# Gated convolution layers: six of eight output blocks by seven half-depth products, and a next layer that begins with two of four chunks

## The chip, the cores and the metric

The kernel runs on one core of a Trainium2 chip. The metric is the device time in microseconds (us) from start to end of one execution; the time given is the median of three runs. Everything is computed in float32.

The engines are called as in the profile: PE multiplies matrices, PEld loads its weights, DVE is the vector engine, ACT the scalar engine, POOL the GpSimd engine, SP an engine that only issues transfers. A name with q (SPq, ACTq) is the engine's queue. Each engine executes its own instructions in the order in which the compiled program has them.

## The reference

The input x is an image of 512 channels and 64 by 64 pixels. Four layers are added to it one after the other, each on the group-normalized image (32 groups of 16 channels, `_gn`):

```
x = x + attention(gn(x))              # layer 0
x = x + gated_convs(gn(x), L1 weights)
x = x + gated_convs(gn(x), L2 weights)
x = x + linear_attention(gn(x))       # layer 3
```

The change is in the two gated layers, and in the seams behind them. A gated layer (channels of `pwa`, `dw0`, `dw1`, `dw2`: 128, 128, 256, 512) is

```
fused  = w_in @ x + b_in              # 1024 x 512
pwa, abc = fused[:128], fused[128:]
dw0, dw1, dw2 = depthwise_7x7(abc) + dw_b
h = pwa * dw0
h = (pw0 @ h + pw0_b) * dw1
h = (pw1 @ h + pw1_b) * dw2
out = w_out @ h + b_out               # 512 x 512
```

The last line, `w_out @ h`, is what the change computes in another way. Layer 3 begins with a 1x1 convolution of the normalized image as well (`w_qkv`, 768 x 512).

## The kernel before, in words

The image X stays in SBUF as four chunks of 128 channels by 4096 pixels; 512 pixels are a block, so there are 8 blocks (`NB`) and 4 chunks (`NC`). A product of one chunk and one block is one matmul of 128 by 128 weights and 512 columns. In float32 the profile records each such matmul twice.

The kernel is written in a language whose scheduler orders instructions from their dependencies and from estimates of their durations. An instruction is placed by hand with `tc.keep_in_program_order`, which puts it behind the last instruction that was traced on the same engine before it. All matmuls that go through `pc.matmul` are placed so: PE follows the order in which the program was traced. Tiles come from pools with a number of buffers; a new tile waits until a buffer of its pool comes free, and a pool of the next layer until what lay there before comes free.

**A gated layer** (`_gated_convs`, once for L1, once for L2). The products of `w_in` are done in pairs of two output chunks and two pixel blocks. `_Seven.steps` does such a pair of pairs in seven products of half depth (two matmuls each) in place of eight, with sums of the weights (`sums`) and differences of the pixels (`differences`, L472); the products p1, p5, p2, p7, p6, p3, p4 follow in this order. Two intermediate results are kept in SBUF (`keep`, on ACT) and added to on DVE (L518, L522). `diff` holds the eight differences of a pair of blocks, in one buffer of the pool `ch` (tiles of 128 by 4096, 5 buffers), from which also the gate `G` and the convolved planes `D[0]` to `D[6]` come.

The seven depthwise convolutions (`convolve(0)` to `convolve(6)`) are done on PE from shifted copies of the planes: each of eight parts of a convolution needs a load of taps (`T`, L1181) and of planes (`S`, L1197) issued by SP, and two copies on ACT (L1204). Two loads are issued ahead, four buffers hold them. Between the parts a list of other products is worked off in order, as many as the number of parts allows: for the last two convolutions these are the gates `g[3]` and `g[4]` (L1475) and the parts of the output product for `D[3]` and `D[4]`, one matmul for each of 8 blocks and 4 output chunks (`output`, L1487 and L1491). When the last convolution is done, `g[5]` and `g[6]` follow and the output product for `D[5]` and `D[6]`, two matmuls each, in the order of the output chunks. As each piece of X is complete, DVE takes its statistics (`bn_stats`, L1493).

**The seam between layers.** The mean and the deviation of a chunk are known when its eight blocks are done. `_Norm.params` combines them in three pieces: the aggregation (L95), a first small matmul with `gmask` (L126) and a second (L135), each followed by small instructions on DVE and ACT. After the second, the factor `r` scales the weights. `centered.take` subtracts the mean from the pixels (L400 on ACT, L401 on the others). The next layer begins in `_first_blocks`, with two output chunks and two blocks, so that three of the four chunks (`NC - 1`) go first: 12 matmuls that need nothing of the last chunk. The pieces for the last chunk are put between them after the fourth and the seventh matmul. Then the last chunk's four matmuls follow.

**The opening of layer 3** (`_linear_attention`). POOL sets the planes of the layer to zero (L1121), issues five transfers into tiles `bt` (L1674) and multiplies four of them (L1680); the result is used later, in `added` (L1684). Then come the scaling of `w_qkv` on DVE (L1693) and `_first_blocks`. Planes are stored by transfers that POOL issues (L1150).

Of the kernel before, what the change touches and what calls it, by code (L numbers as in the profile page):

```python
# [10 lines left out]
FP = mybir.dt.float32  # L11
# [426 lines left out]
class _Seven:  # L438
# [42 lines left out]
    def first(self, a, x, ps):  # L481
        self.multiply(ps, a[:, 0:2], [x(c, 0) for c in range(2)], True)

    def steps(self, a, b, s, t, x, bank, keep, put, early=lambda more, last: None, p1_kept=None):

        nc = self.nc
        ps, kept = {}, {}

        def add(j, w, hs, first):

            if first:
                ps[j] = bank(j)
            self.multiply(ps[j], w, hs, first)

        def p1():
            if p1_kept is not None:
# [12 lines left out]
        def p2():  # L511
            if p1_kept is None:
                add(0, a[:, 2:4], [x(2 + c, 0) for c in range(2)], False)
                put(0, 0, ps[0], None)

        def p7():
            add(2, s[2], t[2], True)
            nc.vector.tensor_add(kept[1], kept[1], ps[2])  # L518

        def p6():  # L520
            add(3, s[1], t[1], True)
            nc.vector.tensor_add(kept[0], kept[0], ps[3])  # L522
            early(kept[0], kept[1])

        def p3():
            add(1, s[3], [x(2 + c, 1) for c in range(2)], False)
            put(0, 1, ps[1], kept[0])

        def p4():
            add(2, b[:, 2:4], t[3], False)  # L530
            put(1, 0, ps[2], kept[0])
            put(1, 1, kept[1], kept[0])

        return [p1, p5, p2, p7, p6, p3, p4]


# [736 lines left out]
                yield  # L1273


def _first_blocks(pc, X, ws, bank, put, pieces, scale, meanwhile):
# [24 lines left out]
    for f in meanwhile:  # L1301
        f()
    for i, k, ps in first:
        add(i, k, ps, NC - 1)
        put(i, k, ps, None)


@with_exitstack
def _gated_convs(ctx, tc, a, X, vcol, vall, gmask, small, new_stats, centered, stats, mv, F):
# [18 lines left out]
    for layer in ("L1", "L2"):  # L1328
# [13 lines left out]
        if norm is None:  # L1342

            norm, ready = _Norm(nc, small, gmask, mv), 0
            centered.by(norm)
            root = wp.tile([1, 1], FP, tag="root", name="root")
            tc.keep_in_program_order(nc.scalar.activation(root, gmask[0:1, 0:1], AF.Sqrt))
            _all(
                norm.params(
                    0, NC, None, bank_gn, centered.first(lambda c: pc.pixels(X[:, c, :], 0))  # L1350
                )
            )
            for c in range(NC):
                centered.scaled(w_in[0], norm.r, nc.vector, c, c + 1, True)
            centered.scaled(w_in[1], norm.r, nc.scalar)
        else:
            ready = NC - 1
# [11 lines left out]
        seven = _Seven(tc, pc.matmul)  # L1369

        def taken(k):
            for c in range(ready if k < 2 else 0, NC):
                centered.take(pc.pixels(X[:, c, :], k), c)

        D = {}

# [53 lines left out]
        def group(i, k):  # L1430
# [7 lines left out]
            def step(n):  # L1438
                if n == 0:
                    if i not in wsum:  # L1440
                        summed(i)
                    steps.extend(
                        seven.steps(
                            w_in[i], w_in[i + 1], wsum[i], diff, view(k), bank,
                            lambda j, ps: keep(i, j, ps),
                            lambda m, n, ps, more: put(i + m, 2 * k + n, ps, more),
                        )
                    )
                    for _ in mine:
                        pass  # L1450
# [11 lines left out]
        def gate(i, b):  # L1462
# [11 lines left out]
                bias = vcol(pre + "pw1_b", i - 3)  # L1474
            nc.vector.scalar_tensor_tensor(d, ps, bias, d, ALU.add, ALU.mult)  # L1475

        def output(chunks, b, o):

            if (b, o) == (0, 0):
                for i in chunks:  # L1480
                    w_out.append(weights("w_out", i - 3))
            ps = product(
                lambda c: w_out[chunks[c] - 3][:, o, :], [D[i][:, ts(b, BLK)] for i in chunks]
            )
            xs = X[:, o, ts(b, BLK)]
            if chunks[0] == 3:
                nc.vector.scalar_tensor_tensor(  # L1487
                    xs, ps, vcol(pre + "b_out", o), xs, ALU.add, ALU.add
                )
            else:  # L1490
                nc.vector.tensor_add(xs, xs, ps)  # L1491
            if chunks[-1] == NDW - 1:
                nc.vector.bn_stats(stats[:, o, b, :], xs)  # L1493


        def blocks(f, i):
            n = (0, 1, 1, 2, 2, 2, 2)[i]
# [54 lines left out]
        _first_blocks(  # L1552
            pc, X, w_in, lambda: ps_mm.tile([P, BLK], FP, tag="mm", name="ps"), put,
            norm.params(ready, NC, old_stats, bank_gn, centered_first) if ready else None,
            scale_last, [] if ready else [lambda: taken(1)],
        )
        centered.began()
        for b in (2, 3):
# [26 lines left out]
        for b, f in enumerate(last[(NC - 1) * NB :]):  # L1585
            f()
            if b in (1, 3):
                next(pieces, None)
        for k in range(2 if layer == "L1" else NB):
            for c in range(NC - 1):  # L1590
                centered.take(_pixels(form, X[:, c, :], k), c)
    return stats, norm

# [2 lines left out]
def _linear_attention(ctx, tc, a, X, vcol, vall, ident, gmask, small, centered, stats, norm, F, Z, out):  # L1596
# [46 lines left out]
    with ExitStack() as st:  # L1643
# [73 lines left out]
            return ps  # L1717

        for i, w in enumerate(w_qkv):
            scaled(i, w, 0, NC - 1)  # L1720
# [58 lines left out]
        def group(i, k, also=()):  # L1779
# [3 lines left out]
            def begin():  # L1783
# [2 lines left out]
                        w_qkv[i], w_qkv[i + 1], wsum[i], diff[k][0], view(k), bank,  # L1786
                        lambda j, ps: keep(i, j, ps),
                        lambda m, n, ps, more: put(i + m, 2 * k + n, ps, more),
                    )
                )  # L1790

# [16 lines left out]
        dve, pool = nc.vector, nc.gpsimd  # L1808

        def centered_first():  # L1810
            tc.keep_in_program_order(
                centered.take(pc.pixels(X[:, NC - 1, :], 0), NC - 1, nc.vector)
            )
            centered.take(pc.pixels(X[:, NC - 1, :], 1), NC - 1)

        def scale_last():
            for i, w in enumerate(w_qkv):
                scaled(i, w, NC - 1)

        _first_blocks(  # L1820
            pc, X, w_qkv, lambda: ps_mm.tile([P, BLK], FP, tag="mm", name="ps"), put,
            norm.params(
                NC - 1, NC, stats,
                lambda: ps_vk.tile([P, BLK], FP, tag="vk0", name="gn_ps"), centered_first,
            ),
            scale_last,
            [lambda: taken(2), lambda: taken(3), lambda: summed(0)] + differences(1, dve),
        )
        centered.began()
        made = group(0, 1, centers(2) + differences(2, dve))  # L1830
# [512 lines left out]
```

## Time and profile before

| what | value |
|---|---|
| median of three runs | 3753.89 us (3752.48 to 3755.92) |
| the profiled execution's own time | 3760.95 us |
| its span, from the first to the last instruction | 3758.9 us |
| granted clock of PE | 0.998 |
| PE busy | 3694.5 us, 98% |
| DVE busy | 2722.7 us, 72% |
| ACT busy | 2067.1 us, 55% |
| POOL busy | 190.3 us, 5% |
| L1: convolution 5 begins, 6 begins, output product ends | 2499.3, 2541.9, 2680.1 us |
| L2: convolution 5 begins, 6 begins, output product ends | 2986.7, 3029.2, 3167.4 us |

A row of a timeline gives the start of a run of equal instructions, how long the run lasted from the start of the first to the end of the last, the engine, the line, the operation, the tiles (out<-in) and their number. What stands in brackets is how long the engine was idle before it, and who released it. A matmul's recorded duration reaches into the next one; the time that a matmul costs is read from the starts. A row of a table by stretches gives the stretch, its length, the busy time of PE, PEld, DVE, ACT and POOL with the number of instructions in brackets, the granted clock of PE, the mean busy share of the 16 DMA engines and what they moved in GB/s.

### The profile page before, as it was taken

What the parts mean: (1) busy time and instruction counts of PE and PEld (TensorE: products, weight loads), DVE (VectorE), ACT (ScalarE), POOL (GpSimd) and SP (SyncE); (2) the same over time, 40 slices, a digit from 0 to 9 for tenths busy, and PEclk for the clock granted to TensorE, in tenths of its full rate; (3) what the DMA queues carried; (4) which work ended last, traced back from release to release, by engine and by line L of the source; (5) the groups of instructions that cost most, each with busy time, mean ns of one, the idle gap of its engine ahead of it and who ended that gap; (6) DMA issues with size and microseconds to landing.
All of it is one profiled execution on the core that took longest, in us unless ns stands there. A gap on an engine that the chain in (4) does not pass through costs nothing. (4 is left out here: it accounts for less than half of the span.)

```text
span 3758.9 us, 81698 instructions
## 1 busy us (share of the span) xinstructions
PE 3694.5 (98%) x35112; PEld 1716.1 (46%) x35112; DVE 2722.7 (72%) x3548; ACT 2067.1 (55%) x3002; POOL 190.3 (5%) x170
## 2 busy tenths in 40 slices
PE   7999999999999999999999999999999999999999
PEld 6544444444464444444333344554444544445543
DVE  6677777777766777778778757776777678666538
ACT  3577774777735777747557546662356632355210
POOL 1000000000000000010000000000000002232112
PEclk9999999999999999999999999999999999999999
DMA  2000000000000000000000026762066631564312
GB/s 102 10 7 7 4 7 12 7 4 7 7 4 10 7 7 4 7 12 7 4 4 7 4 76 199 197 185 60 23 182 187 191 89 41 157 180 104 99 56 93
DMA packets 183469, 222.72 MB, mean 59 GB/s; under 512 B 15800, under 2 KB 124600, under 8 KB 182976
## 3 DMA queue, kind: packets, MB, share of 16 engines
q1 hardware_dynamic: 158896, 158.62, 15.7%
q10 hardware_dynamic: 21168, 47.77, 3.5%
q0 software_dynamic: 3040, 11.08, 0.8%
q8 instruction: 277, 4.54, 0.5%
q14 instruction: 88, 0.72, 0.1%
HBM read 157.51 MB, written 59.90 MB: 58 GB/s over the span
## 5 line engine op out<-in xcount | busy, mean ns | idle before, releaser
L844 ACT ACTIVATE pt<-ps_s,A 128x512 f32<-128x512 f32 x2048 | 1286.1, 688 | 447.1 <-PE ps_s L836 436.9
L836 PE MATMUL ps_s<-O,K 64*64 64x512 f32 x8192 | 1419.8, 589 | 0.0
L1017 DVE TENSOR_TENSOR acc<-acc,pt 128x1024 f32<-128x1024 f32 x960 | 1177.5, 1227 | 324.6 <-ACT pt L844 298.7
L856 PE MATMUL av<-pt,O 64*64 64x512 f32 x4096 | 747.0, 589 | 0.0
L856 PE MATMUL av<-pt,V 64*64 64x512 f32 x4096 | 674.3, 589 | 0.0
L836 PEld LDWEIGHTS ps_s<-O,K 64*64 64x64 f32 x8192 | 438.8, 133 | 513.3 <-issue 463.2
L1204 ACT COPY S<-S 32x1295 f32<-32x1295 f32 (+1 forms) x272 | 341.8, 1257 | 228.7 <-DMA S<-F 137.3
L856 PEld LDWEIGHTS av<-pt,O 64*64 64x64 f32 x4096 | 238.0, 133 | 250.5 <-issue 237.7
L856 PEld LDWEIGHTS av<-pt,V 64*64 64x64 f32 x4096 | 210.1, 133 | 266.9 <-issue 252.1
L1127 PEld LDWEIGHTS ps_cv<-S,T 64*32 64x32 f32 x13824 | 194.0, 105 | 115.7 <-issue 72.5
L1127 PE MATMUL ps<-diff,w_sum 128*128 128x512 f32 x516 | 242.0, 601 | 3.5 <-DVE w_sum L459 2.9
L1127 PE MATMUL ps_cv<-S,T 64*32 64x128 f32 x13824 | 234.6, 273 | 9.0 <-issue 4.2
L1127 PE MATMUL ps<-h,w_out_L 128*128 128x512 f32 x512 | 229.6, 600 | 1.6 <-DVE X L1487 1.4
L472 DVE TENSOR_TENSOR diff<-X 128x512 f32<-128x512 f32 x200 | 134.9, 691 | 68.0 <-PE ps L1127 36.1
L400 ACT ACTIVATE X<-X,gn_less 128x512 f32<-128x512 f32 x118 | 75.3, 709 | 153.7 <-DVE gn_less L130 153.0
L1127 PE MATMUL ps<-X,w_in_L 128*128 128x512 f32 x304 | 146.2, 612 | 10.9 <-ACT kept L1409 7.8
L1127 PEld LDWEIGHTS ps<-diff,w_sum 128*128 128x128 f32 x516 | 94.6, 190 | 117.3 <-issue 104.0
L1127 PEld LDWEIGHTS ps<-h,w_out_L 128*128 128x128 f32 x512 | 94.0, 190 | 118.3 <-issue 96.5
L1127 PE MATMUL ps<-h,pw_L 128*128 128x512 f32 x320 | 144.3, 600 | 3.0 <-DVE h L1475 2.8
L1258 DVE STREAM_TRANSPOSE h<-ps_cv 128x512 f32<-128x512 f32 x112 | 109.2, 1048 | 52.3 <-PE ps_cv L1127 52.0
L472 DVE TENSOR_TENSOR diff<-X,diff 128x512 f32<-128x512 f32 x200 | 135.3, 685 | 11.6 <-PE ps L1127 11.5
L1127 PE MATMUL ps<-agg,w_proj 128*128 128x512 f32 x256 | 117.2, 595 | 1.6 <-DVE turned L1258 1.6
(265 smaller groups left out, 3354.2 us busy)
## 6 DMA issues: line engine op xcount, KB each, us to landing
T<-in_L_T_dram SPq DMA_DIRECT2D x112, 384.0 KB, 4.2
F<-plane ACTq DMA_DIRECT2D x112, 324.0 KB, 3.5
S<-F SPq DMA_DIRECT2D x224, 162.0 KB, 4.7
S<-G SPq DMA_DIRECT2D x96, 153.0 KB, 4.5
row<-G SPq DMA_DIRECT2D x48, 272.0 KB, 3.4
T<-in_L_T_dram SPq DMA_DIRECT2D x48, 256.0 KB, 4.2
G<-plane POOLq DMA_DIRECT2D x33, 289.0 KB, 2.7
rd<-R SPq DMA_DIRECT2D x64, 128.0 KB, 2.9
```

The costliest lines, as they stand in the source:

```text
L400: return self.nc.scalar.activation(xs, xs, AF.Identity, bias=less)
L472: yield eng.tensor_tensor(t[j][c], a(c), b(c), ALU.subtract)
L836: nc.tensor.matmul(ps[ts(half, D), ts(h, BLK)], K[rows, t * P + half * D : t * P + (half + 1) * D], QO[pair][rows, cols], start=True, stop ...
L844: exp = nc.scalar.activation(pt[:, ts(h, BLK)], ps[:, ts(h, BLK)], AF.Exp, bias=A[:, t, h : h + 1])
L856: nc.tensor.matmul(av[half][rows, :], v[keys, t * P + h * D : t * P + (h + 1) * D], pt[keys, ts(h, BLK)], start=(t == 0), stop=(t == NT - 1),)
L1017: add = nc.vector.tensor_add(acc, acc if u > 1 else first, pt)
L1127: self.tc.keep_in_program_order(self.nc.tensor.matmul(*args, **kw))
L1204: nc.scalar.copy(second, first)
L1258: nc.vector.transpose(out, src)
```

## The change

In both gated layers the output product is no longer split by the depth of `D`, with one part behind each of the last convolutions, for all blocks. Blocks 0 and 1 are done as before, behind the same convolutions. Blocks 2 to 7 are done after them, as three pairs of blocks with all four of `D[3]` to `D[6]`, by `_Seven.steps` for two output chunks at a time (`outputs_by_seven`). The sums of `w_out` are made on POOL, the differences on DVE, the kept results are copied by ACT. Where a result has a second summand, POOL adds it to X (in the last group of all DVE does), and then DVE takes the statistics. `w_out` is loaded as four tiles by output chunk instead of by depth, before convolution 5. Because `D[3]` to `D[6]` now all live to the end, the pool `ch` has six buffers.

Chunks 2 and 3 of X are now complete only at the end of the last group. So the next layer begins with two chunks (`READY`) instead of three: 8 matmuls, then, in place of the four that are missing, the first products (p1) of the groups that follow (`begin_two` in L2 for two groups, `begin_one` in layer 3 for one), then 8 matmuls of chunks 2 and 3. The centering of the first two chunks is prepared for the blocks 0, 1, 2 and 4 (`FIRST`) in L2. Chunk 2 of the first block is centered on POOL, chunk 3 on DVE; in layer 3 POOL centers chunk 2 of the later blocks too.

```diff
@@ _Seven.steps, p1
-            ps[0] = bank(0)
-            self.first(a, x, ps[0])
+            if given is None:
+                ps[0] = bank(0)
+                self.first(a, x, ps[0])
+            else:
+                ps[0] = given
             kept[0] = keep(0, ps[0])
@@ _first_blocks
-    for n, (i, k, ps, c) in enumerate((*p, c) for p in first for c in range(NC - 1)):
+    for n, (i, k, ps, c) in enumerate((*p, c) for p in first for c in range(READY)):
         add(i, k, ps, c)
         if n in (3, 6):
             next(pieces, None)
+    early()
     scale()
     for f in meanwhile:
         f()
     for i, k, ps in first:
-        add(i, k, ps, NC - 1)
+        for c in range(READY, NC):
+            add(i, k, ps, c)
         put(i, k, ps, None)
+READY = 2
+FIRST = (0, 1, 2, 4)
@@ _gated_convs
-    hp = ctx.enter_context(tc.tile_pool(name="ch", bufs=5))
+    hp = ctx.enter_context(tc.tile_pool(name="ch", bufs=6))
...
+        def begin_two():
+            for k in (1, 2):
+                begun[k] = ps_cv.tile([P, BLK], FP, tag="mm", name="ps7")
+                seven.first(w_in[0], view(k), begun[k])
...
+        def load_out():
+            for o in range(NC):
+                t = w2p.tile([P, NC, P], FP, tag="w", name=f"w_out_{layer}")
+                nc.sync.dma_start(
+                    out=t, in_=a[f"{layer}_w_out"][:, :, o].rearrange("c p m -> p c m")
+                )
+                w_out.append(t)
...
+        def outputs_by_seven(ks):
+            diff = hp.tile([P, N], FP, tag="h", name="diff")
+            diff = [[diff[:, ts(2 * j + c, BLK)] for c in range(2)] for j in range(4)]
+            rest = hp.tile([P, N], FP, tag="h", name="rest")
...
+            for m in range(2):
+                _all(seven.sums(nc.gpsimd, w_out[2 * m], w_out[2 * m + 1], sums[m]))
...
+            for k in ks:
...
+                made = seven.differences(nc.vector, view, diff)
+                for m in range(2):
+                    def add(i, n, first, more):
+                        o, b = 2 * m + i, 2 * k + n
+                        xs = X[:, o, ts(b, BLK)]
+                        nc.vector.scalar_tensor_tensor(
+                            xs, first, vcol(pre + "b_out", o), xs, ALU.add, ALU.add
+                        )
+                        if more is not None:
+                            eng = nc.vector if (k, m) == (ks[-1], 1) else nc.gpsimd
+                            eng.tensor_tensor(xs, xs, more, ALU.add)
+                        nc.vector.bn_stats(stats[:, o, b, :], xs)
...
+                    for n, step in enumerate(steps):
+                        if m == 0:
+                            for _ in range((2, 2, 2, 0, 2, 0, 0)[n]):
+                                next(made)
+                        step()
+                        yield
...
-                (n, lambda b=b, o=o: output(chunks, b, o)) for b in range(NB) for o in range(NC)
+                (n, lambda b=b, o=o: output(chunks, b, o)) for b in range(2) for o in range(NC)
...
         def centered_first():
-            tc.keep_in_program_order(
-                centered.take(pc.pixels(X[:, NC - 1, :], 0), NC - 1, nc.vector)
-            )
-            centered.take(pc.pixels(X[:, NC - 1, :], 1), NC - 1)
+            for c in range(READY, NC):
+                tc.keep_in_program_order(
+                    centered.take(
+                        pc.pixels(X[:, c, :], 0), c, nc.vector if c == NC - 1 else nc.gpsimd
+                    )
+                )
+            for c in range(READY, NC):
+                centered.take(pc.pixels(X[:, c, :], 1), c)
...
         convolve(4, [], b56[16:])
+        load_out()
         convolve(5, g[3], outputs(3))
         convolve(6, [], g[4] + outputs(4))
-        for _, f in g[5] + g[6]:
-            f()
-        last = [lambda b=b, o=o: output((5, 6), b, o) for o in range(NC) for b in range(NB)]
-        for f in last[: (NC - 1) * NB]:
+        for _, f in g[5] + g[6] + outputs(5, 6):
             f()
         norm = _Norm(nc, small, gmask)
         centered.by(norm)
-        pieces = norm.params(0, NC - 1, stats, bank_gn)
-        next(pieces)
+        pieces = norm.params(0, READY, stats, bank_gn)
+        ks = range(1, NB // 2)
+        for n, _ in enumerate(outputs_by_seven(ks)):
+            if n - (14 * len(ks) - 7) in (1, 3, 4):
+                next(pieces, None)
@@ _linear_attention
         def taken(k):
-            centered.take(pc.pixels(X[:, NC - 1, :], k), NC - 1)
+            for c in range(READY, NC):
+                centered.take(pc.pixels(X[:, c, :], k), c, nc.gpsimd if c < NC - 1 else None)
...
+        def begin_one():
+            begun.append(bank(0))
+            seven.first(w_qkv[0], view(1), begun[0])
```

In layer 3 `centered_first` has the same form as in the gated layers, the weights are scaled in two steps of two chunks, and the small matmuls of the normalization take the bank `vk3` instead of `vk0`.

More of the change, by code (lines that the diff above doesn't have):

```diff
@@ L482, in first, with steps @@
         self.multiply(ps, a[:, 0:2], [x(c, 0) for c in range(2)], True)
-    def steps(self, a, b, s, t, x, bank, keep, put, early=lambda more, last: None, p1_kept=None):
+    def steps(self, a, b, s, t, x, bank, keep, put, early=lambda more, last: None, p1_kept=None,
+              given=None):
         nc = self.nc
@@ L1273, in conv, with _first_blocks @@
                 yield
-def _first_blocks(pc, X, ws, bank, put, pieces, scale, meanwhile):
+def _first_blocks(pc, X, ws, bank, put, pieces, scale, meanwhile, early):
     first = [(i, k, bank()) for k in range(2) for i in range(2)]
@@ L1356, in _gated_convs @@
         else:
-            ready = NC - 1
+            ready = READY
             for w in w_in[:2]:
@@ L1371, in taken @@
         def taken(k):
-            for c in range(ready if k < 2 else 0, NC):
+            for c in range(ready if k in FIRST else 0, NC):
                 centered.take(pc.pixels(X[:, c, :], k), c)
+        begun = {}
+        def begin_two():
+            for k in (1, 2):
+                begun[k] = ps_cv.tile([P, BLK], FP, tag="mm", name="ps7")
+                seven.first(w_in[0], view(k), begun[k])
         D = {}
@@ L1446, in step @@
                             lambda m, n, ps, more: put(i + m, 2 * k + n, ps, more),
+                            given=begun.pop(k, None),
                         )
@@ L1475, in gate @@
             nc.vector.scalar_tensor_tensor(d, ps, bias, d, ALU.add, ALU.mult)
+        def load_out():
[5 more added lines that the diff above has]
+                w_out.append(t)
         def output(chunks, b, o):
-            if (b, o) == (0, 0):
-                for i in chunks:
-                    w_out.append(weights("w_out", i - 3))
             ps = product(
-                lambda c: w_out[chunks[c] - 3][:, o, :], [D[i][:, ts(b, BLK)] for i in chunks]
+                lambda c: w_out[o][:, chunks[c] - 3, :], [D[i][:, ts(b, BLK)] for i in chunks]
             )
@@ L1493, in output, with keep, view, put @@
                 nc.vector.bn_stats(stats[:, o, b, :], xs)
+        def outputs_by_seven(ks):
+            diff = hp.tile([P, N], FP, tag="h", name="diff")
+            diff = [[diff[:, ts(2 * j + c, BLK)] for c in range(2)] for j in range(4)]
+            rest = hp.tile([P, N], FP, tag="h", name="rest")
+            sums = rest[:, 0 : N // 2].rearrange("p (m n c k) -> p m n c k", m=2, n=4, c=2)
+            rows = [rest[:, ts(n, BLK)] for n in range(NB // 2, NB)]
+            sums = [[sums[:, m, n] for n in range(4)] for m in range(2)]
+            for m in range(2):
+                _all(seven.sums(nc.gpsimd, w_out[2 * m], w_out[2 * m + 1], sums[m]))
+            def keep(j, ps):
+                t = rows.pop(0)
+                rows.append(t)
+                nc.scalar.copy(t, ps)
+                return t
+            for k in ks:
+                def view(c, n):
+                    return D[3 + c][:, ts(2 * k + n, BLK)]
+                made = seven.differences(nc.vector, view, diff)
[10 more added lines that the diff above has]
+                        nc.vector.bn_stats(stats[:, o, b, :], xs)
+                    def put(i, n, ps, more):
+                        if (i, n) != (1, 1):
+                            add(i, n, ps, more)
+                    steps = seven.steps(
+                        w_out[2 * m], w_out[2 * m + 1], sums[m], diff, view, bank, keep, put,
+                        lambda more, last: add(1, 1, last, more),
+                    )
[5 more added lines that the diff above has]
+                        yield
         def blocks(f, i):
@@ L1542, in centered_first @@
         def centered_first():
-            tc.keep_in_program_order(
-                centered.take(pc.pixels(X[:, NC - 1, :], 0), NC - 1, nc.vector)
-            )
-            centered.take(pc.pixels(X[:, NC - 1, :], 1), NC - 1)
+            for c in range(READY, NC):
[3 more added lines that the diff above has]
+                    )
+                )
+            for c in range(READY, NC):
+                centered.take(pc.pixels(X[:, c, :], 1), c)
         def scale_last():
@@ L1554, in _gated_convs @@
             norm.params(ready, NC, old_stats, bank_gn, centered_first) if ready else None,
-            scale_last, [] if ready else [lambda: taken(1)],
+            scale_last, [] if ready else [lambda: taken(1)], begin_two,
         )
@@ L1581, in _gated_convs @@
         centered.by(norm)
-        pieces = norm.params(0, NC - 1, stats, bank_gn)
-        next(pieces)
-        form = FORM if layer == "L1" else FORM3
[L1585 to L1590, printed above, removed]
+        pieces = norm.params(0, READY, stats, bank_gn)
[3 more added lines that the diff above has]
+                next(pieces, None)
+        form = FORM if layer == "L1" else FORM3
+        for k in FIRST if layer == "L1" else range(NB):
+            for c in range(READY):
                 centered.take(_pixels(form, X[:, c, :], k), c)
@@ L1719, in _linear_attention @@
         for i, w in enumerate(w_qkv):
-            scaled(i, w, 0, NC - 1)
+            scaled(i, w, 0, READY)
         def taken(k):
-            centered.take(pc.pixels(X[:, NC - 1, :], k), NC - 1)
+            for c in range(READY, NC):
+                centered.take(pc.pixels(X[:, c, :], k), c, nc.gpsimd if c < NC - 1 else None)
         def put(i, k, ps, more=None):
@@ L1788, in begin @@
                         lambda m, n, ps, more: put(i + m, 2 * k + n, ps, more),
+                        given=begun.pop() if begun else None,
                     )
@@ L1810, in centered_first @@
         def centered_first():
[L1811 to L1814, printed above, removed]
+            for c in range(READY, NC):
+                tc.keep_in_program_order(
+                    centered.take(
+                        pc.pixels(X[:, c, :], 0), c, nc.vector if c == NC - 1 else nc.gpsimd
+                    )
+                )
+            for c in range(READY, NC):
+                centered.take(pc.pixels(X[:, c, :], 1), c)
         def scale_last():
             for i, w in enumerate(w_qkv):
-                scaled(i, w, NC - 1)
+                scaled(i, w, READY)
+        begun = []
+        def begin_one():
+            begun.append(bank(0))
+            seven.first(w_qkv[0], view(1), begun[0])
         _first_blocks(
@@ L1822, in _linear_attention @@
             norm.params(
-                NC - 1, NC, stats,
-                lambda: ps_vk.tile([P, BLK], FP, tag="vk0", name="gn_ps"), centered_first,
+                READY, NC, stats,
+                lambda: ps_vk.tile([P, BLK], FP, tag="vk3", name="gn_ps"), centered_first,
             ),
@@ L1827, in _linear_attention @@
             [lambda: taken(2), lambda: taken(3), lambda: summed(0)] + differences(1, dve),
+            begin_one,
         )
```

## The prediction

> **What bounds the kernel now.** I read the page first, then the tensor engine's timeline around the end of a gated layer, then the timelines of the engines that feed it there.
>
> ```profile
> span 3758.9 us, 81698 instructions
> PE 3694.5 (98%) x35112; PEld 1716.1 (46%) x35112; DVE 2722.7 (72%) x3548; ACT 2067.1 (55%) x3002; POOL 190.3 (5%) x170
> ```
>
> PE is the bound, so work taken off it counts in full unless a gap opens. The sum is made against this execution (span 3758.9, its own time 3760.95); the unprofiled runs have a median of 3753.89, 7 us less, and I subtract the difference from that median. Under 0.2% (7.5 us) I call it no change.
>
> The stretch that is rewritten, on PE, where L1 ends (T0, the last output product, is 2680.1) and L2 begins:
>
> ```profile
> 2624.71 44.80 PE L1127 MATMUL ps<-h,w_out_L 128*128 128x512 f32 x104
> 2669.34 0.28 PE L126 MATMUL gn_ps<-gn_mv,gmask 128*128 128x3 f32 x2
> ...
> 2673.14 7.11 PE L1127 MATMUL ps<-h,w_out_L 128*128 128x512 f32 x16
> 2680.09 3.60 PE L1127 MATMUL ps<-X,w_in_L 128*128 128x512 f32 x8
> 2683.52 0.28 PE L126 MATMUL gn_ps<-gn_mv,gmask 128*128 128x1 f32 x2
> ```
>
> No gap: the next layer's first products hide the normalization. One matmul of 512 columns is two records; eight records take from 2680.09 to 2683.52, so a matmul costs 0.86 us.
>
> The same seam on DVE, and, between L2 and L3 (T0 there 3167.4), on POOL:
>
> ```profile
> 2681.01 0.69 DVE L1493 BATCH_NORM_STATS2 stats<-X 128x6 f32<-128x512 f32 x1
> 2681.74 0.37 DVE L95 BATCH_NORM_AGGREGATE gn_mv<-stats 128x2 f32<-128x48 f32 x1
> ```
>
> ```profile
> 3167.67 4.23 POOL L1121 MEMSET plane<- 128x578 f32 x8 [973.13 <-PE ps L1127]
> 3171.85 2.40 POOL L1674 DMA_DIRECT2D bt<-in_L_w_projT_dram  x4
> 3174.24 0.54 POOL L1674 DMA_DIRECT2D bt<-in_L_bt_dram  x1
> 3178.92 16.42 POOL L1680 TENSOR_TENSOR bt<-bt 128x512 f32<-128x512 f32 x4 [4.14 <-DMA bt<-in_L_bt_dram]
> ```
>
> DVE has the last statistics 2 us after T0, and PE asks for them at T0+3.4. POOL opens L3 with 28 us of work that nothing urgent waits for.
>
> **The change: products.** A layer's output has 32+32+64=128 matmuls. After: 8+8+16=32 for blocks 0 and 1, and 3 pairs x 2 output pairs x 7 products x 2=84 for the rest. 12 fewer, 10.3 us a layer, 20.6 us for two. A rule matters here: the Trainium skill, "Trainium Kernel Development and Optimization", section Performance Expectations, calls matmul busy time a bad metric because matmuls are pipelined. The page's mean of a record is 600 ns, which would make 48 records 28.8 us; by the starts it is 20.6. I take the starts.
>
> **Convolutions 5 and 6 lose filler.** Convolution 5 had three output matmuls between parts, now three in four parts. The window of one part:
>
> ```profile
> 2526.80:2531.10 4.30, 4.30 (x103) 2.39 (x103) 2.40 (x4) 2.54 (x2) 0.00 (x0) 1.00 0.64 173
> ```
>
> A part needs 4.30x0.64=2.75 us of all DMA engines and 2.54 us of ACT copies. PE will need 1.53+0.65=2.2 us. Four loads are ready when it starts; of the next four, three are then short by about 0.5 us each: 1.6 us a layer. Bounds: 0 (the late loads are covered), 4 (DMA at the 86% share that 2416 to 2446 shows). The gaps of 0.72 us at the end of convolution 5 (PE waiting for L1487) go, since the additions that caused them do. Convolution 6 keeps some 3.4 us of PE a part and stays PE's. Net of both, 0.9 us a layer lost. SP: all four w_out loads are now traced before convolution 5's loads; the old ones were issued at 2384, 2399, 2477 and 2482, as buffers came free, wherever they were traced, so I cost the move at nothing: what hides it is PE's work until the first output product at 2500.8. If SP held convolution 5's loads behind them, each would cost its 256 KB, by the window above 2.75x256/708=1 us, 4 us a layer; the smaller pieces that the new layout is read in (512 bytes) can add to that, and no row shows by how much.
>
> **The seven-product stage, 72 us a layer.** Per pair of blocks (24.1 us of PE) DVE does 8 differences, 4 kept additions, 8 scaled additions, 8 statistics: 28 at 0.60 to 0.66 us apart, 17.7 us. ACT's 12 copies a layer and POOL's 8 weight sums lie beside 13.7 us of products. POOL does six additions a pair, and the statistics queued on DVE behind each wait for it. Alone such an addition took 1.27 us; in L3's tail eight took 12.54 and a DVE difference beside them went from 0.69 to 1.71; the four of L1680 took 4.1 each. The skill, "SBUF — State Buffer", section on the two separate sides, calls the shared port an exclusive lock, so that one POOL addition should wait for one DVE instruction, about 0.69+1.27=2 us; L1680 says 4.1. With 1.6 us (the tail's row, a seven-product stage too) and 1.0 us more for three or so differences, DVE needs 17.7+3+some unfilled waits, under 24.1. Four PSUM buffers give slack: the one of the sixth product is wanted again by the second product of the next group, 3.4 us after its own end, that of the seventh 5.1 us after. Cost 0.5 us a layer; 0 and 10 as ends.
>
> **Seam to L2.** Now two chunks, not one, are measured late. After PE's fifth product of the last group DVE has ten instructions of some 0.63, 1 us of small ones and two aggregations: it ends at about T0+4.5, where PE asks at T0+3.4. With the first scaled weights up to 1 us late, 2 us lost; ends 0 and 5. Chunk 2 is centered by POOL (1.73 us for that in L1's opening) beside PE's begun products. Those are moved, not added.
>
> **Seam to L3.** The centering of chunk 2, block 0 is put on POOL and pinned behind the last thing traced there: L1680. PE, in order, reaches that chunk after 8 products and 2 begun ones, T0+8.6. POOL: 2.9 us of DMA issue, 4.1 to landing, four multiplications, 1.73 of centering. As before it also has 4.2 us of memsets first; with a sixth `h` buffer the planes of convolutions 3 and 4 come free 10 us before T0, so I take the memsets as done by then. Multiplications: two undisturbed at 1.3, two slowed by DVE's weight scaling and sums, 8.8 together. 2.9+4.1+8.8+1.7=T0+17.5, so PE stands 8.9 us, which contains the later statistics. Lower end 3 (rows loaded early); upper end 21 (memsets at T0, 4.1 each). Queued behind it: PE's whole stream, the second differences on DVE, and POOL's own plane stores, none of them urgent sooner. The gaps of 0.20 and 0.63 us at 3171 and 3196 vanish, 0.8 back.
>
> **Sum.** 20.6-1.8-1.0-2.0-8.9+0.8=7.7 us faster, 3753.9-7.7=3746.2, so 3746.
>
> **The rivals.**
> A, the above. Its own range is 2 to 14 us faster, 3740 to 3752, from L3's stall (8.9, minus 4, plus 4) and convolution 5. Chance 0.50, of which 0.32 beyond 0.2%.
>
> B, POOL's chain in L3 is as slow as now: stall 21 in place of 8.9 gives 3746+12=3758. For it: 16.42 us for four multiplications. Against: DVE will itself wait for centered chunks and leave POOL the port. Chance 0.20, of which 0.09 beyond 0.2% slower.
>
> C, slower: DVE waits for POOL in the seven-product stage. It decides once the waits and slowed differences exceed 24.1-17.7=6.4 us a pair, or 1.07 for each POOL addition. At 1.5 each the excess is 2.6 us a pair, 16 us for six, and the sum is +8: 3762; at 4.1 each it would be over 100. For it: the row of 4.1, and statistics stand in order behind each addition. Against: L3's tail has products, additions on POOL and differences side by side, and PE lost only 1.9 us there; the waits can be filled with the next pair's differences. Chance 0.15. The skill's "GPSIMD Engine Reference", section 4.1, would put these additions on VectorE: 6x0.65 more gives 21.6 us a pair, still under 24.1 and without that risk.
>
> D, L3's rows arrive early and convolution 5 never waits: 3 in place of 8.9 and 1.6 twice regained, 16.8 us faster, 3737. Chance 0.15.
>
> That it doesn't save products is excluded by the count above.
>
> **How the numbers follow.** Faster by over 0.2%: 0.32+0.15=0.47. Slower: 0.09+0.15=0.24. No change: the rest, 0.29. The range goes past D by the lower end of the seam to L2 (2 us) and of the stages (1), and past C's 3762 by the upper end of that seam: 3733 to 3766; C's worse ends are left out.
>
> **What would show it.** On PE, after the 16 matmuls of blocks 0 and 1, 84 matmuls in 72 us without a gap above 1 us: C is wrong; if instead PE waits for L518, L522 or the new additions, with DVE idle behind POOL, C is right. In L3 a single PE gap of 6 to 12 us behind the eight first products and the two begun ones, released by POOL's centering (L401), itself behind L1680: A; above 15, B; under 4, D. In convolution 5 PE waits on ACT's S copies by 1 to 3 us. At L2 a gap of 1 to 3 us at L126. A total loss in the stage before T0 would make the prediction wrong; so would a DVE that ends later than T0+7.

## The result, and the profile after

| | before | after |
|---|---|---|
| median of five runs beside each other | 3755.92 us | 3774.11 us |
| ratio, 95% interval | | 1.005 (1.0039 to 1.0062) |
| span of the profiled execution | 3758.9 us | 3772.3 us |
| granted clock of PE in it | 0.998 | 0.995 |

Slower by about 18 us, where 8 us faster was forecast, and above the range (3733 to 3766). The first lines of the page, of after:

```profile
span 3772.3 us, 81699 instructions
PE 3683.3 (98%) x35064; PEld 1716.1 (45%) x35064; DVE 2718.9 (72%) x3530; ACT 2073.6 (55%) x3017; POOL 249.5 (7%) x224
```

48 PE records are gone, 24 a layer, as counted; PE is busy 11.2 us less and the span is 13.4 longer. So PE stands 24.6 us more than it did. Where, I read from PE's timeline, by stage. T0 is again the end of a layer's last output product, and "p5" is the first product of a pair by sevens in the next layer. The lines of after are numbered 4 higher up to the new code.

| stage | before | after | difference |
|---|---|---|---|
| up to convolution 5 of L1 | 2499.3 | 2500.8 | +1.5 |
| L1, convolution 5 to T0 | 180.8 | 183.3 | +2.5 |
| seam to L2 (T0 to p5) | 15.9 | 19.2 | +3.3, of which 1.7 is a product moved there |
| L2, p5 to convolution 5 | 290.6 | 282.5 | -8.1, of which 1.7 is that product |
| L2, convolution 5 to T0 | 180.8 | 183.2 | +2.4 |
| seam to L3 (T0 to p5) | 16.3 | 32.4 | +16.1 |
| the rest of L3 | 575.2 | 570.9 | -4.3 |

Two rows carry it. From convolution 5 to T0, 10.3 us of products are gone and the stage is still some 2.5 longer: about 12.8 us are lost in it, in each layer. And the seam to L3 is 16 us longer. The two rows with a gain are mostly small gaps in stages whose products the change leaves as they are: in the first part of L2 they add up to 11.2 us in before, 5.0 here, and 5.8 to 11.4 in the profiled runs below; in the rest of L3 to 13.4 in before and 11.7 here, and before runs 3.4 us of that stage at half clock, after none. I count neither as a gain of the change.

**Convolution 5 and the start of 6**, on PE. In before every part (96 records) is followed by three output products, and no part waits:

```profile
2522.30 2.84 PE L1127 MATMUL ps<-h,w_out_L 128*128 128x512 f32 x6
2525.08 1.59 PE L1127 MATMUL ps_cv<-S,T 64*32 64x128 f32 x96
```

In L1 of after:

```profile
2508.68 1.50 PE L1131 MATMUL ps_cv<-S,T 64*32 64x128 f32 x83 [0.88 <-issue]
2514.20 1.08 PE L1131 MATMUL ps_cv<-S,T 64*32 64x128 f32 x54 [2.15 <-issue]
2518.52 0.65 PE L1131 MATMUL ps_cv<-S,T 64*32 64x128 f32 x25 [0.96 <-issue]
2522.68 1.65 PE L1131 MATMUL ps_cv<-S,T 64*32 64x128 f32 x93 [0.82 <-issue]
2534.93 2.79 PE L1131 MATMUL ps_cv<-S,T 64*32 64x128 f32 x88 [3.42 <-ACT S L1208]
2537.64 3.47 PE L1131 MATMUL ps<-h,pw_L 128*128 128x512 f32 x4
2541.04 1.59 PE L1131 MATMUL ps_cv<-S,T 64*32 64x128 f32 x96
```

The bracket is the idle time ahead of a group. Four gaps within convolution 5 are 4.8 us together, and 5.1 with one of 0.27 in the first part of convolution 6; "issue" says only that the profile shows no releaser. In the second part of convolution 6 PE stands 3.42 us for a copy that ACT makes of a plane. After that stop it is slow: 88 small products in 2.79 us where 96 take 1.59, and four records in 3.47 where four take 1.98. The windows of the same stretches (us of each engine busy, then granted clock, DMA share, GB/s):

```profile
2506.00:2511.00 5.00, 4.12 (x195) 3.06 (x194) 2.45 (x5) 2.54 (x2) 0.00 (x0) 1.00 0.96 241
2511.00:2516.00 5.00, 2.85 (x99) 1.73 (x98) 1.58 (x3) 4.22 (x4) 0.00 (x0) 1.00 1.04 201
2535.00:2541.00 6.00, 6.00 (x92) 3.41 (x92) 1.96 (x2) 5.90 (x5) 0.00 (x0) 0.53 0.36 108
```

In the first two, all DMA engines are busy, and ACT, which copies each plane as it lands, waits for DMA as well:

```profile
2506.79 2.56 ACT L1208 COPY S<-S 32x1295 f32<-32x1295 f32 x2 [2.91 <-DMA S<-F]
2511.04 2.56 ACT L1208 COPY S<-S 32x1295 f32<-32x1295 f32 x2 [1.69 <-DMA S<-F]
```

So the gaps stand for the loads of planes and taps. In the third window the granted clock is 0.53: the products after the stop run at half clock. Why ACT was late, ACT's timeline shows:

```profile
2527.88 1.15 ACT L1591 ACTIVATE h<-h,vec 128x1024 f32<-128x1024 f32 x1 [4.81 <-DVE h L1268]
2529.06 1.27 ACT L1208 COPY S<-S 32x1295 f32<-32x1295 f32 x1
2530.36 3.23 ACT L1591 ACTIVATE h<-h,vec 128x1024 f32<-128x1024 f32 x3
2533.61 11.61 ACT L1208 COPY S<-S 32x1295 f32<-32x1295 f32 x9
```

L1591 adds the bias to `D[5]`, the plane that convolution 5 has just made; it waits 4.81 us for DVE to transpose it (L1268). The two copies for the second part of convolution 6 stand behind it in ACT's order, the second of them behind the other three biases too; PE goes on when that one ends, at 2534.9. L2 has the same stop, of 4.01 us.

**The seven-product stage** has no PE gap at all in L1, and PE is busy 63.86 of 64 us in it. **The seam to L2** has one gap of 1.34 us, for weights scaled on ACT (L407), not at L126 as forecast.

**The seam to L3**: PE, then POOL, then DVE.

```profile
3171.71 5.37 PE L1131 MATMUL ps<-X,w_qkv 128*128 128x512 f32 x8 [2.58 <-DVE w_qkv L1768]
3177.05 2.82 PE L1131 MATMUL ps<-X,w_qkv 128*128 128x512 f32 x6
3179.85 2.82 PE L1131 MATMUL ps<-X,w_qkv 128*128 128x512 f32 x6
3192.89 8.67 PE L1131 MATMUL ps<-X,w_qkv 128*128 128x512 f32 x16 [10.22 <-POOL X L401]
```

```profile
3171.33 4.22 POOL L1125 MEMSET plane<- 128x578 f32 x8 [10.29 <-DVE X L1552]
3175.50 2.36 POOL L1749 DMA_DIRECT2D bt<-in_L_w_projT_dram  x4
3177.85 0.54 POOL L1749 DMA_DIRECT2D bt<-in_L_bt_dram  x1
3178.42 7.96 POOL L401 TENSOR_SCALAR X<-X,gn_less 128x512 f32<-128x512 f32 x5
3186.35 4.91 POOL L1755 TENSOR_TENSOR bt<-bt 128x512 f32<-128x512 f32 x4
3191.25 3.62 POOL L401 TENSOR_SCALAR X<-X,gn_less 128x512 f32<-128x512 f32 x2
```

```profile
3171.96 1.92 DVE L1768 SCALAR_TENSOR_TENSOR w_qkv<-w_qkv,gn_r,s_qkv 128x128 f32<-128x128 f32 x7
3182.36 9.75 DVE L1768 SCALAR_TENSOR_TENSOR w_qkv<-w_qkv,gn_r,s_qkv 128x128 f32<-128x128 f32 x8
```

The 10.22 us end with POOL's centering of block 0, and POOL's list shows why it is late. But DVE's scaling of chunks 2 and 3 of `w_qkv`, without which PE cannot go on either, ends at 3192.1 too: eight instructions in 9.75 us, where seven of the same form take 1.92 shortly before, with POOL on its memsets. And each of the two gaps is followed by slow products: 5.37 for eight records that take 3.60 in before, 8.67 for sixteen that take 7.11. 2.58 + 10.22 + 1.77 + 1.56, less the gap of 0.20 of before, is 15.9 of the 16.1 us.

### The profile page after: what moved, and what is told of

Same layout as the page of the kernel before. It is cut to its first block, busy times and chain, and to the rows that moved or that the text cites. A ratio compares the mean times of both kernels' runs of the same rounds, so it can differ in the third digit from the quotient of the medians.

```text
span 3772.3 us, 81699 instructions
## 1 busy us (share of the span) xinstructions
PE 3683.3 (98%) x35064; PEld 1716.1 (45%) x35064; DVE 2718.9 (72%) x3530; ACT 2073.6 (55%) x3017; POOL 249.5 (7%) x224
## 5 line engine op out<-in xcount | busy, mean ns | idle before, releaser
L1131 PE MATMUL ps_cv<-S,T 64*32 64x128 f32 x13824 | 237.8, 274 | 24.6 <-issue 12.7
L1533 ACT COPY rest<-ps 128x512 f32<-128x512 f32 x24 | 14.0, 585 | 191.4 <-PE ps L1131 191.4
L1131 PE MATMUL vkp<-kT,vT 128*128 128x512 f32 x256 | 115.2, 592 | 0.0
L1493 DVE SCALAR_TENSOR_TENSOR h<-ps,vec,h 128x512 f32<-128x512 f32 x96 | 70.8, 745 | 60.5 <-PE ps L1131 59.9
```

Source lines behind the costliest of these rows:

```text
L1131: self.tc.keep_in_program_order(self.nc.tensor.matmul(*args, **kw))
L1533: nc.scalar.copy(t, ps)
```

## The experiments

I held four readings against each other. F: convolutions 5 and 6 lack filler, since six of eight blocks of output products have left them. Q: only ACT's order is at fault (the biases of `D[5]` ahead of the copies). P: at L3 it is block 0's place in POOL's queue. S: at L3 it is POOL working beside DVE, which slows the scaling. Each ratio is to runs of the kernel before made beside the run; the medians of these differ by some 2 us, so I compare ratios. Layer times are of the profiled executions.

**Filler back: gates moved into the convolutions.** The gates of `D[4]` and `D[5]`, which do not depend on the change, are put between the parts one convolution earlier.

```diff
-        convolve(5, g[3], outputs(3))
-        convolve(6, [], g[4] + outputs(4))
+        convolve(5, g[3], g[4] + outputs(3))
+        convolve(6, [], g[5] + outputs(4))
-        for _, f in g[5] + g[6] + outputs(5, 6):
+        for _, f in g[6] + outputs(5, 6):
```

> The changed kernel, with the gates g[4] moved from convolution 6 into convolution 5 and g[5] from behind convolution 6 into it: the same instructions, only PE's filler between the parts is moved. Theory F (filler: the loads of a convolution cannot keep up once PE needs only 2.2 us a part, and the gap lowers PE's clock): the 6 us of gaps in convolution 5, the 3.4 us at the start of convolution 6 and the half clock behind it (3 us) go, 8 to 12 us a layer, 16 to 24 us in all, to about 3754. Rival Q (ACT's queue holds the first S copy of convolution 6 behind the biases of D[5], whatever the filler): only convolution 5's gaps go, 4 to 6 us a layer, to about 3764.

3760.82 us, ratio 1.0005 (0.9996 to 1.0014): against after's 1.005 that is 0.45%, 17 us of the loss are back. PE's gaps in convolutions 5 and 6 of L1 are 0.66, 0.24, 0.58 and 0.34 us, none of over 0.24 for ACT's copies, and the parts of convolution 5 ran at full clock with PE busy all of the time:

```profile
2504.00:2531.00 27.00, 27.00 (x800) 15.96 (x788) 12.53 (x15) 17.58 (x15) 0.00 (x0) 1.00 0.69 184
```

From convolution 5 to T0 this version takes 172.2 us in L1 and 173.4 in L2, where before takes 180.8 in both. So 8.6 and 7.4 of the 10.3 us of products arrive once PE has something to do while it waits; gaps of 2.1 and 2.8 us, in place of 0.7, take most of the rest. The seam to L3 is unchanged (gaps of 2.58 and 10.24 us). The median lies between what F (3754) and Q (3764) expected; the gaps speak for F. But ACT's order changed with the edit as well (two copies now stand between two pairs of biases), so this run alone does not rule Q out.

**The bias of `D[5]` on POOL**, all else as after.

```diff
+                if i == 5:
+                    nc.gpsimd.tensor_scalar(t, t, vcol(pre + "dw_b", i), None, ALU.add)
+                    return
                 nc.scalar.activation(t, t, AF.Identity, bias=vcol(pre + "dw_b", i))
```

> The changed kernel, with the bias of D[5] (four instructions behind convolution 5) added by POOL instead of ACT, so that ACT's S copies for convolution 6 stand behind nothing that waits for DVE. Theory Q (the order of ACT's queue makes the gap of 3.4 us at the start of convolution 6): the gap falls below 1 us and PE's clock stays at full speed, 5 to 6 us a layer, about 3763. Rival D (the loads come late from DMA): the gap stays above 2.5 us, under 2 us a layer gained.

3769.96 us, ratio 1.0033 (1.0018 to 1.0048). PE in L1:

```profile
2515.83 1.07 PE L1131 MATMUL ps_cv<-S,T 64*32 64x128 f32 x54 [2.43 <-issue]
2533.41 0.89 PE L1131 MATMUL ps_cv<-S,T 64*32 64x128 f32 x42 [0.67 <-issue]
```

The stop in convolution 6 falls from 3.42 to 0.67 and the slow products behind it are gone; in L2 it falls from 4.01 to 2.11, and they are not. The larger gaps within convolution 5 stay: 2.43 us in L1, 2.64 in L2, both with slow products behind them. By the ratios some 6 us are gained, of the 17 that the gates bring back. So Q is one part of the loss and not the whole: it is what missing filler lets through to PE.

**The same loss without any seven-product stage.** In the kernel before, the output products of `D[3]` and `D[4]` for blocks 2 to 7 are moved behind convolution 6 (with six `ch` buffers); the number of products is as before.

```diff
-        def outputs(*chunks):
+        def outputs(*chunks, bs=range(2)):
...
-        for _, f in g[5] + g[6]:
+        later = range(2, NB)
+        for _, f in outputs(3, bs=later) + outputs(4, bs=later) + g[5] + g[6]:
             f()
```

> The kernel before, with only the place of its output products for D[3] and D[4] changed: for blocks 2 to 7 they run behind convolution 6 instead of between the parts of convolutions 5 and 6 (six buffers of the pool ch, as in the change). No product by seven, the next layer begins with three chunks. Theory F: the same gaps as in the changed kernel appear, 11 to 13 us a layer, about 3779. If the loss in the changed kernel has another cause (the seven products' own loads, sums or waits): within 5 us of the kernel before.

3788.44 us, ratio 1.0077 (1.006 to 1.0094), so about 29 us for moving products alone; F expected 11 to 13 a layer. From convolution 5 to T0 it takes 195.6 us in L1 and 196.4 in L2, 14.8 and 15.6 longer than before. PE in L1 (this kernel has before's line numbers):

```profile
2508.24 1.50 PE L1127 MATMUL ps_cv<-S,T 64*32 64x128 f32 x83 [0.88 <-issue]
2515.67 1.92 PE L1127 MATMUL ps_cv<-S,T 64*32 64x128 f32 x54 [4.06 <-issue]
2536.31 2.78 PE L1127 MATMUL ps_cv<-S,T 64*32 64x128 f32 x88 [4.04 <-ACT S L1204]
```

The same places, the same halved clock after each stop of 4 us. It is the move, not the new arithmetic, that costs; this is the clearest run for F. The sixth buffer is no rival: the run with the gates has it too, without the loss.

**Block 0 of chunk 2 on DVE in L3**, POOL's other centering left.

```diff
-                        pc.pixels(X[:, c, :], 0), c, nc.vector if c == NC - 1 else nc.gpsimd
+                        pc.pixels(X[:, c, :], 0), c, nc.vector
```

> The changed kernel, with chunk 2 of block 0 centered by DVE instead of POOL in layer 3 alone. Theory P (the pinned centering behind POOL's four multiplications is what PE waits for): the gap of 10.2 us shrinks to 1 to 3 us, and the half clock behind it goes: 8 to 10 us faster than the changed kernel, about 3765. Rival S (DVE's scaling of w_qkv, 9.75 us for eight beside POOL's centering, would be as late): the gap stays at 7 us or more, within 3 us of the changed kernel.

3774.96 us, ratio 1.0044 (1.003 to 1.0059): no gain that can be told from after. PE at the seam:

```profile
3193.17 7.13 PE L1131 MATMUL ps<-X,w_qkv 128*128 128x512 f32 x16 [1.37 <-DVE w_qkv L1768]
3203.54 1.97 PE L1131 MATMUL ps<-diff,w_sum 128*128 128x512 f32 x4 [3.24 <-DVE diff L472]
```

The gap of 10.2 is now 1.37 and 3.24, and from T0 to p5 it is 25.4 us, 7 less. DVE's second scaling still takes 9.49 us, and the differences of the first pair stand in order behind it. Later gaps of 1.11 and 3.05 us (after has one of 1.20) take back about 3 of the 7, and half clock for 6.8 us around the second of them about 3 more. The profiled execution is the slowest of its five, 9 us over the median, so this need not hold for the others. A miss for P alone: the place in the queue was what the wait ended on, with the scaling right behind it.

**All of chunk 2's centering in L3 off POOL** (block 0 to DVE, the others to ACT).

```diff
-                centered.take(pc.pixels(X[:, c, :], k), c, nc.gpsimd if c < NC - 1 else None)
+                centered.take(pc.pixels(X[:, c, :], k), c)
...
-                        pc.pixels(X[:, c, :], 0), c, nc.vector if c == NC - 1 else nc.gpsimd
+                        pc.pixels(X[:, c, :], 0), c, nc.vector
```

> The changed kernel, but all of layer 3's early centering of chunk 2 is taken from POOL (block 0 to DVE, the others to ACT); POOL keeps the memsets, the five transfers and the four bt multiplications. Theory S (POOL's work beside DVE's scaling of w_qkv slows both; the centering is its larger part): DVE's second scaling, eight instructions in 9.75 us before, now meets only the multiplications (4.9 us of POOL, from about T0+9), so about 4 us; T0 to the first p5 shrinks from 32.4 to about 22 and it is kept later, 3764. Theory P (only the place of block 0 in POOL's queue counts): the scaling stays at 9 us or more, T0 to p5 is 25 as in the run with block 0 alone on DVE, and nothing is gained in the total: 3774.

3770.06 us, ratio 1.0037 (1.0024 to 1.0051). DVE's scaling and POOL's multiplications, at the same time:

```profile
3183.99 6.26 DVE L1768 SCALAR_TENSOR_TENSOR w_qkv<-w_qkv,gn_r,s_qkv 128x128 f32<-128x128 f32 x8
```

```profile
3184.47 5.11 POOL L1755 TENSOR_TENSOR bt<-bt 128x512 f32<-128x512 f32 x4 [3.86 <-DMA bt<-in_L_bt_dram]
```

The scaling shrinks only to 6.26 us, but it is no longer in PE's way: T0 to p5 is 20.8 us, 11.6 less than in after. The total gained less than that: this profiled execution, the fastest of its five, has a span 8.5 us shorter; the ratios put the gain at about 5 us, and their intervals overlap. Its convolution 5 still has the gaps and the slow products, and they differ from one execution to the next (in this one slow products also follow a gap of 2.46 us within it, which after does not have), so I don't split the remainder.

**Gates, and the bt multiplications later.** The filler is back, seven centerings stay on POOL, and the multiplications are pinned behind the first plane stores.

```diff
...
-        for t in w_bt:
-            nc.gpsimd.tensor_tensor(t, t, bt, ALU.mult)
         def added():
+            for t in w_bt:
+                tc.keep_in_program_order(nc.gpsimd.tensor_tensor(t, t, bt, ALU.mult))
```

> The gates among the parts as before, and only the bt multiplications pinned behind the first plane stores; seven centerings stay on POOL, in a row. By theory S they still stand beside DVE's second scaling: it stays at 8 to 10 us; block 0's centering ends about 4.9 us sooner, so the gap goes from 10.2 to 5 to 8, and the total is 3756 to 3759. By theory P the multiplications ahead of it are 4.9 us of the stall and come off whole: gap 5, total 3756. If the multiplications alone are what slows the scaling, it falls to about 3 us, which neither says.

3747.91 us, ratio 0.9975 (0.9964 to 0.9986): 11 us better than the gates alone, where at most 5 were expected. POOL, DVE and PE:

```profile
3156.65 11.55 POOL L401 TENSOR_SCALAR X<-X,gn_less 128x512 f32<-128x512 f32 x7
```

```profile
3159.93 4.24 DVE L1767 SCALAR_TENSOR_TENSOR w_qkv<-w_qkv,gn_r,s_qkv 128x128 f32<-128x128 f32 x8
```

```profile
3160.74 7.11 PE L1131 MATMUL ps<-X,w_qkv 128*128 128x512 f32 x16 [1.54 <-DVE w_qkv L1767]
```

What I had overlooked: block 0's centering is pinned behind what was traced last on POOL. With the multiplications gone from that place nothing holds it back (PE begins the sixteen products when two of the seven centerings are done), and PE no longer waits for POOL there. Five centerings ahead of it in after were not a decision about centering; they were put in front of the multiplications, and block 0 had to stay behind these. So one edit takes away the place in the queue (P) and most of the slowing (S): beside centering alone the scaling takes 4.24 us, and PE's gap is 1.54.

**All three repairs**: gates, no centering on POOL in L3's opening, the multiplications later.

> All three repairs: the gates g[4] and g[5] among the parts of convolutions 5 and 6, no centering on POOL in layer 3's opening, and the bt multiplications pinned behind the first plane stores. By theory S nothing of POOL stands beside DVE's second scaling: eight in 2.2 us, no 10 us gap, T0 to p5 about 20 us (16.3 as before the change, 1.7 for the two products begun early, 2 to 3 for the late first scaling). That is 12 us under the run with the gates alone (3760.8): 3749, 8 faster than before. By theory P the gain is at most the 7 us that moving block 0 brought at the seam, and is lost again later: 3758 to 3761.

3744.57 us, ratio 0.9966 (0.9953 to 0.9978). With POOL silent, the same eight instructions:

```profile
3156.74 2.19 DVE L1767 SCALAR_TENSOR_TENSOR w_qkv<-w_qkv,gn_r,s_qkv 128x128 f32<-128x128 f32 x8
```

T0 to p5 is 20.3 us, as expected, although for another reason than the text gives: 1.7 us of it are not a product begun early but eight records at reduced clock (5.28 in place of 3.60) behind a gap of 2.60. The total cannot be told from the run before, since the intervals overlap; what POOL does to the scaling is read from the rows. S holds: 9.75 us beside both, 6.26 beside the multiplications, 4.24 beside centering, 2.19 alone.

**The first two chunks' parameters earlier**, on top of the three repairs.

```diff
-            if n - (14 * len(ks) - 7) in (1, 3, 4):
+            if n - (14 * len(ks) - 7) in (0, 2, 3):
...
-                            eng = nc.vector if (k, m) == (ks[-1], 1) else nc.gpsimd
+                            eng = nc.vector if k == ks[-1] else nc.gpsimd
```

> The version with all three repairs, and the parameters of the first two chunks earlier: their three pieces stand behind the first, third and fourth product of the last group (not the second, fourth and fifth), and the last pair's additions are all on DVE. If the stop at both seams (1.34 us in front of L2, 2.6 in front of L3) is only the late chain of pieces, it moves forward by one product of 1.72 us: gap 0 at L2, under 1 us at L3, and the eight records behind it in L3 take 3.6 us, not 5.3: 4 to 5 us off, ratio to before 0.9954. If DVE's own queue at the end of the last group sets it (additions, statistics, then the scaling), the chain waits there instead, the gaps stay at 1 to 3 us, and the ratio stays 0.9966.

3739.18 us, ratio 0.9962 (0.9948 to 0.9976): the best version, by the ratio 14 us faster than before. That is against before; against the version without the edit the intervals overlap, and only the profile shows the gain. The gap at L2 is gone, and at L3 PE shows:

```profile
3143.80 1.88 PE L1131 MATMUL ps<-X,w_qkv 128*128 128x512 f32 x4
3146.53 1.98 PE L1131 MATMUL ps<-X,w_qkv 128*128 128x512 f32 x4 [0.85 <-DVE w_qkv L1767]
```

0.85 and later 0.53 us in place of 2.60, no slow products, T0 to p5 17.8 us. Which of the two edits did it was not separated.

## Why the prediction was wrong, step by step

- **12 products a layer, 20.6 us: right.** 48 records are gone, and with filler in place the time from convolution 5 to T0 falls by 8.6 and 7.4 us, to which gaps add 1.4 and 2.1: 10.0 and 9.5 of the 10.3. Counting starts and not the 600 ns of a busy record was the right reading.
- **"Net of both, 0.9 us a layer lost": the step that failed first.** It was 12.8, and a sign that the prediction itself gave of being wrong, a total loss in the stage before T0, is there: 2.5 us a layer. Three terms. The loads: three late by 0.5 us, 1.6 in all, came from 2.75 us of DMA a load, scaled up from a window with a share of 0.64. With the engines full (0.96 and 1.04) a load of 708 KB (of 1024 bytes) at 241 and 201 GB/s takes 3.0 to 3.6 us, so each was later, and the gaps are 5.1 us, over the upper bound of 4 too. ACT: the prediction weighed ACT's sum (2.54 us of copies a part) and not its order, in which four biases, the first waiting 4.8 us for DVE, stand among the copies for convolution 6's second part; "Convolution 6 keeps some 3.4 us of PE a part and stays PE's" missed this: 3.4 and 4.0 us. The clock: nothing was set down for what a stop does to the products behind it, 2.8 us in L1. With the tail gaps of 0.59 and 0.34 and less the 0.72 that went, that makes 11.5; 1.3 us I cannot place.
- **Weights' loads, nothing: right.** SP issued two of them at 2478.6 and 2483.7; before had two at 2477.1 and 2482.2.
- **Seven-product stage, 0.5 us: it cost nothing.** Rival C is out. POOL's additions took mostly 1.27 us. In each of L1's first two pairs DVE's statistics waited four times for one, 0.7 to 1.4 us and 4.9 together, under the 6.4 that C needs, and PE did not stand.
- **Seam to L2, 2.0 us: 1.6,** but the gap is at the first scaled weights. The factors for these come from the late statistics; with their chain one product earlier and the last pair's additions on DVE it was gone, and which of the two removed it is open.
- **Seam to L3, 8.9 us less 0.8: the second step that failed.** 16.1, by 15.9 us of gaps and slow products. The mechanism and the place were named (POOL's L401 behind the multiplications), and the gap of 10.2 lies in the 6 to 12 given, but partly by luck: T0+17.5 for its end was T0+23.9, from errors that partly cancel: the memsets, taken as done before T0, began at T0+2.4, when the last addition had read the buffer `rest` (6.5 us late together with their 4.2; that it is this buffer which they wait for is read from the code); five centerings of 7.96 us went ahead of the multiplications, which the sum did not have; against that, the multiplications took 4.9 in place of 8.8, and no wait for the rows was left. By the trace: 2.4+4.2+2.9+7.9+4.9+1.6=23.9. The sum also took 8.6 us for PE's arrival; PE came at 13.7, later by the first gap and the slow clock, which is why the gap was not 15. DVE's scaling, slowed beside POOL to 9.75 us, would have held PE nearly as long and was not in the sum.
- **Chances.** Slower by over 0.2% had 0.24, for POOL reasons (B and C). The main cause, PE without work in convolution 5 and 6, was set down as a small term in every case, so no rival held it.

## What to carry to other kernels

Work that is moved out of a stage with transfers and copies takes away the cover of everything that was late there; before costing such a move, list each engine's order at that place, not its busy sum, and find other independent work to put in the hole (here gates, which brought back 17 us). A saving on the bound engine counts only after the waits it uncovers have been priced one by one, and a wait of 2 us or more may be followed by 3.4 us or more at half clock. An instruction pinned "behind the last" on a queue inherits whatever stands there: move that away, and both it and its neighbours go free.

## What the runs showed of the hardware

- **A stop of some 2 to 3 us can halve PE's clock, and the same stop need not.** After gaps of 2.15 (after, L1), 2.27 (gates alone, L2) and 3.17 us (no centering on POOL, convolution 5 of L2) the clock stayed at 1.00. After 2.17 (output products moved, L2) it was 0.50, after 2.46 (no centering on POOL, L1) 0.52, and after 2.58 (after, seam to L3) 0.68 over the next 5.3 us. One stop of 1.96 to 1.99 us at the same place in L2 was followed by half clock in two of the eight traces that have it (after, and gates with later multiplications). Behind each of the eight stops of 3.4 to 4.1 us in the two layers the clock was 0.50 to 0.59 over the first us.
- **Half clock comes in whole pieces.** In the ten traces it lasts 3.41 us (34 times), 6.83 (13) or 10.24 (9), never a length between, but for the last piece of each, at the program's end. So one piece costs at most some 1.7 us of products, an estimate by halving 3.41. The Trainium skill, "TensorE: Matmul & The Clock Gate", section "What's actually happening", says that activity is judged in a free-running window of 3413 ns; the lengths agree with it, and that one and the same gap goes both ways agrees with a window whose phase is not the program's, but stops well under its length were enough.
- **DVE beside POOL can stand for a whole run of POOL's instructions.** In after one of the eight scalings, of 0.34 us alone, lasted 5.8 us, over all four multiplications back to back (4.91 us); in the run without POOL's centering the longest was 1.36 us, about one multiplication. Both were seen; what decides between them was not tested. Centering, with one input in SBUF, slowed the scaling by a factor of two (4.24 against 2.19 for eight).
